# A routed block's last three expert tiles behind a branch, and another order of combining

## The chip, the core and the metric

The kernel runs on one core of a Trainium2 chip. The metric is the device time of one launch in microseconds. TensorE (PE; its weight loads are PEld) multiplies, VectorE (DVE) and ScalarE (ACT) do the elementwise work and read PSUM, GpSimd (POOL) does elementwise work in SBUF and issues the indirect DMAs, SyncE (SP) issues all other DMAs.

## The reference

A transformer block in float32 with a modulation by a condition vector: layer norm, attention with 16 heads, a residual, layer norm again, then a mixture of experts with a shared expert beside it. x has 4 batches of 512 tokens of 512 features. Cut to what matters:

```python
x = x + ga * attn(layernorm(x) * (1 + ca) + sa)
h = layernorm(x) * (1 + cb) + sb                  # 2048 tokens x 512
scores = softmax(h @ gate_weight.T)               # 8 experts
topk_w, topk_idx = top_k(scores, 2)               # two experts a token
topk_w = topk_w / (sum(topk_w) + 1e-20)
y  = sum over the two experts of topk_w * (silu(h @ wg.T) * (h @ wu.T)) @ wd.T   # F = 352
y += (silu(h @ sg.T) * (h @ su.T)) @ sd.T                                        # shared, FS = 704
x = x + gb * y
```

## The kernel before

**Sorting by expert.** The attention part fills the first two thirds of the time and is left as it is. While it runs, `route(b)` finds each token's two experts and scatters the token's row to `xs` in DRAM, which has a region for each expert; `xs` was filled with zeros before, in 15 pieces (line 1151, `xs<-nothing`), one after each head from the second on. At the end `plan_tiles` counts the tokens of each expert and cuts each expert's region into tiles of 128 rows. `ends[e]` is the running sum of tiles over the experts; `expert_of[i]` and `row_of[i]` say which expert's weights and which row of `xs` tile i takes. 4096 rows in 8 groups need at most 39 tiles (`NT`), and the program always runs 39: tiles behind the counted ones take the last expert and rows of zeros, and nobody reads what they give.

**A tile.** `load_in(i)` reads the expert's number into a register of SP and loads its gate and up weights into `wgu[i % 2]` (line 1418), `load_down(i)` its down weights into `wdn[i % 2]` (line 1434); both are conditional: where tile i has the expert of tile i - 2 nothing is loaded. `load_rows(i)` loads 128 rows. On PE `tile_in` transposes them (pxt, line 1443), `tile_hidden` multiplies by gate and up (pgt and put, line 1456), ACT and DVE make the product of silu and up, `tile_turn` transposes it (pht, line 1472), `tile_down` multiplies by the down weights (pyt, line 1483), ACT copies the result to `yt` (line 1491), and `keep(i)` writes it to `ys` in DRAM (line 1495). The loop is pipelined by hand: in pass i PE gets tile i's hidden products, tile i + 1's transposes, tile i - 1's down and tile i's second transposes, so that ACT and DVE work on one tile while PE works on another.

**The shared expert.** It runs in two halves of two batches, one before the tiles and one behind them. Each half begins with `shared_tail` for both of its batches (64 of the hidden columns that don't fit the blocks: pst, line 1204, then a silu on ACT, line 1212, and two products on DVE, line 1215, into `hid`), goes on with `shared_hidden` for five blocks (w_s, line 1229) and ends with `shared_down` for each of its two batches (w_d, line 1310). Hidden and down products use seven products in place of eight (`seven`); each is taken from PSUM by DVE or ACT before its bank can be used again. These banks, the tag "w", are three in number; pst and the tiles' pgt use the same three. In the second half a down's quadrants are added to the residual on DVE, multiplied by gb and sent to the output from there (lines 1332 to 1336).

**Combining.** `combine(n, bt)` takes a block of 128 tokens: `fetch` gathers its two rows from `ys` by indirect DMAs on POOL, four blocks ahead. For batches 0 and 1 the two rows are weighted and multiplied by gb and added to the residual, by ACT (line 1529), DVE (1531, 1532) and POOL (1533), and SP sends the block (`finish`, line 1499). For batches 2 and 3 two DVE instructions (1525, 1527) add the weighted rows to a residual that has been divided by gb ahead of time, and it goes out later, with the second half's downs. The combining is a generator of two steps a block, woven between the steps of the second half's products: 24 steps during the hidden products, 8 during the downs. Batches 0 and 1 share one place in SBUF for their residuals (`xr1`), so batch 1's is loaded when batch 0 has left.

**Order.** PE, DVE, ACT and SP run in the order of the program text (`manual_schedule`); POOL's order is the scheduler's. The pools of the stages ("half1", "tiles", "half2") lie over one another in SBUF: `hid` of the second half lies where `xT`, `ht`, `hTt` and `yt` of the tiles were.

Of the kernel before, what the change touches and what calls it, by code (L numbers as in the profile page):

```python
# [14 lines left out]
P = 128  # L15
# [21 lines left out]
TOPK = 2  # L37
CAP = B * S
NT = TOPK * B * S // P + NE - 1
NFILL = 15  # L40
NROW = NE * CAP + (NE - 1) * P
I32 = mybir.dt.int32
# [6 lines left out]
def adaln_block_kernel(  # L49
# [29 lines left out]
    def bank(tag, name):  # L79
        if tag in ("ps", "pt"):  # L80
            return psum.tile([P, 512], F32, tag=tag, name=name)
        bufs = {"w": 3, "po": 1}[tag]
        return psum2.tile([P, 512], F32, tag=tag, bufs=bufs, name=name)
# [328 lines left out]
    def plan_tiles(shp):  # L412


        late["plan"] = []

        def t(tag, *dims, dt=F32):
            return shp.tile([P, *dims], dt, tag=tag, name=tag)

        def over(a, n):  # L420
            return a.unsqueeze(1).to_broadcast([P, n, a.shape[1]])

        def each(a, n):
            return a.unsqueeze(2).to_broadcast([P, a.shape[1], n])

        pn = bank("pt", "pn")[:, :NE]
        nc.tensor.matmul(pn, lhsT=ones, rhs=seen[:, B * NTB, :], start=True, stop=True)
        count = t("count", NE)
        nc.vector.tensor_copy(count, pn)
        begun = t("begun", NE, B * NTB)  # L430
        nc.vector.tensor_tensor(
            begun, each(count, B * NTB), over(full, NE), ALU.is_gt
        )
        tiles = t("tiles", NE)
        nc.vector.tensor_reduce(tiles, begun, AX.X, ALU.add)
        yield
        upto = t("upto", NE, NE)
        nc.vector.tensor_tensor(upto, ltri, over(tiles, NE), ALU.mult)
        ends = t("ends", NE)
        nc.vector.tensor_reduce(ends, upto, AX.X, ALU.add)  # L440
        yield
        past = t("past", NT, NE)
        nc.vector.tensor_tensor(past, each(tileno, NE), over(ends, NT), ALU.is_ge)
        which = t("which", NT)
        nc.vector.tensor_reduce(which, past, AX.X, ALU.add)
        nc.vector.tensor_scalar_min(which, which, float(NE - 1))
        expert_of = t("expert_of", NT, dt=I32)
        nc.vector.tensor_copy(expert_of, which)
        yield
        step = t("step", NE)  # L450
        nc.vector.tensor_scalar(
            step, tiles, float(-P), float(CAP), op0=ALU.mult, op1=ALU.add
        )
        nc.vector.tensor_tensor(past, past, over(step, NT), ALU.mult)
        nc.vector.tensor_reduce(which, past, AX.X, ALU.add)
        nc.vector.scalar_tensor_tensor(
            which, tileno, float(P), which, op0=ALU.mult, op1=ALU.add
        )
        row_of = t("row_of", NT, dt=I32)
        nc.vector.tensor_copy(row_of, which)  # L460
        late["plan"] = [expert_of, row_of]
        yield

        move = t("move", NE)
        nc.vector.tensor_sub(move, ends, tiles)
        nc.vector.scalar_tensor_tensor(
            move, move, float(P), slot0, op0=ALU.mult, op1=ALU.subtract
        )
        nc.vector.tensor_add(at, at, over(move, B * NTB))
        rows = []  # L470
        late["plan"].append(rows)
        for k in range(TOPK):
            yield
            mine, row, found = t("mine", B * NTB, NE), t("row", B * NTB), t(f"rows{k}", B * NTB, dt=I32)
            nc.vector.tensor_mul(mine, hots[k], at)
            nc.vector.tensor_reduce(row, mine, AX.X, ALU.add)
            nc.vector.tensor_copy(found, row)
            rows.append(found)
# [374 lines left out]
    def load_for_second(b):  # L853

        late["x"] = work.tile([P, NTB, D], F32, tag="xh", bufs=1, name=f"xh_2_{b}")
        nc.sync.dma_start(out=late["x"], in_=x[b].rearrange("(t p) d -> p t d", p=P))
        spread(ga_bc, GA, b)
        late["mod"] = [
            work.tile([P, D], F32, tag=f"rows{k}", bufs=1, name=f"rows{k}_{b}")
            for k in range(2)  # L860
        ]
        spread(late["mod"][0], CB, b)
        spread(late["mod"][1], SB, b)
# [135 lines left out]
    def weave(main, n, fill, count):  # L999

        done = 0
        for k in range(n):
            next(main, None)
            while done * n < count * (k + 1):
                done += 1
                next(fill, None)
# [50 lines left out]
    with tc.manual_schedule(engines={ENG.PE, ENG.DVE, ENG.Activation, ENG.SP}):  # L1057
# [15 lines left out]
        for G in range(NGB):  # L1073
# [14 lines left out]
            for u in range(GH):  # L1088
# [56 lines left out]
                    open_out(b)  # L1145
                if (g, u) == (3, 2):
                    load_for_second(b)

                k, n = GH * G + u - 1, NROW // P // NFILL
                if 0 <= k < NFILL:  # L1150
# [46 lines left out]
    def halves2(a):  # L1197
        return a.rearrange("p b (s n) -> p b s n", s=2)

    def shared_tail(b):  # L1200

        pt = bank("w", f"pst_{b}")
        for c in range(NC):
            nc.tensor.matmul(
                pt,
                lhsT=wst[:, c, :],
                rhs=h2s[b][:, c // 2 * 2 : c // 2 * 2 + 2, c % 2, :],
                start=(c == 0),
                stop=(c == NC - 1),
            )  # L1210
        sg = gate[:, b % 2]
        nc.scalar.activation(sg[FT:, :], pt[:FT, :], AF.Silu)
        for k in range(2):
            rows = slice(FT + k * FT // 2, FT + (k + 1) * FT // 2)
            nc.vector.tensor_mul(
                hids[b // 2 * 2][FT:FL, b % 2, k::2, 1, :],
                halves(sg[rows]),
                halves(pt[rows]),
            )
# [185 lines left out]

    def other(i):

        if i < 2:
            return {}
        return dict(  # L1410
            cond=expert[i] != expert[i - 2]
        )
# [34 lines left out]
        nc.vector.tensor_copy(xT.rearrange("p c s -> p (c s)"), pt)  # L1447
        return xT

    def tile_hidden(i, xT):  # L1450
        pg = bank("w", f"pgt_{i}")
        pu = bank("ps", f"put_{i}")
        for k, ps in enumerate((pg, pu)):
            for c in range(NC):
                at = (k * NC + c) * F
                nc.tensor.matmul(  # L1456
                    ps[:, :F],
                    lhsT=xT[:, c, :],
                    rhs=wgu[i % 2][:, at : at + F],
                    start=(c == 0),  # L1460
                    stop=(c == NC - 1),
                )
        sg = phase[-1].tile([P, F], F32, tag="tsg", name=f"tsg_{i}")
        nc.scalar.activation(sg, pg[:, :F], AF.Silu)
        ht = phase[-1].tile([P, F], F32, tag="ht", name=f"ht_{i}")
        nc.vector.tensor_mul(ht, sg, pu[:, :F])
        return ht
# [26 lines left out]
    def keep(i, yt):  # L1494
        nc.sync.dma_start(out=ys[i * P : (i + 1) * P, :], in_=yt)
# [54 lines left out]
    with tc.manual_schedule(engines={ENG.PE, ENG.DVE, ENG.Activation, ENG.SP}):  # L1550
# [17 lines left out]
        open_phase("half1")  # L1568
        load_xr(0, moe, "xr0")
        open_hidden(0)  # L1570
        shared_tail(0)
        sums_of_b(nc.gpsimd, h2s[0])
        shared_tail(1)
        sums_of_b(nc.vector, h2s[1])

        def slots_found():
# [28 lines left out]
        open_phase("tiles")  # L1605
        turned = {0: tile_in(0, xts.pop(0))}
        flat, ready = {}, divided()
        for i in range(NT + 1):
            if i < NT:
                ht = tile_hidden(i, turned.pop(i))  # L1610
                if i + 2 < NT:
                    load_in(i + 2)
                    xts[i + 2] = load_rows(i + 2)
                if i + 1 < NT:
                    turned[i + 1] = tile_in(i + 1, xts.pop(i + 1))
            if i >= 1:
                yt = tile_down(i - 1, flat.pop(i - 1))
                if i + 1 < NT:
                    load_down(i + 1)
                keep(i - 1, yt)  # L1620
            if i < NT:
                flat[i] = tile_turn(i, ht)
            next(late["steps"], None)
            if i == 4:
                load_h2(2)
                load_h2(3)
            if i >= 6:
                next(ready, None)
            if i == 8:
                most_of_b(nc.gpsimd, h2s[2])  # L1630
                most_of_b(nc.gpsimd, h2s[3])


        open_phase("half2")
        order = [bt for b in (0, 2, 3, 1) for bt in range(b * NTB, (b + 1) * NTB)]
        open_hidden(2)
        load_xr(0, moe, "xr1")
        shared_tail(2)
        shared_tail(3)
        rest_of_b(nc.gpsimd, h2s[2])  # L1640
        rest_of_b(nc.gpsimd, h2s[3])
        for m in range(4):
# [1 line left out]

        def combined():
            for m, bt in enumerate(order):
                if m == 3 * NTB:
                    load_xr(1, moe, "xr1")
                yield from combine(m, bt)
                if m + 4 < len(order):  # L1650
                    fetch(m + 4, order[m + 4])
                yield
# [2 lines left out]
        weave(main, 4, iter(()), 0)  # L1655
        weave(main, NSEV - 6, fill, 6 * NTB)
        weave(main, 5, iter(()), 0)
        weave(main, 2 * SEVEN - 2, fill, 2 * NTB)
        drain(main)
        drain(fill)  # L1660
        parts.close()
# [112 lines left out]
```

## Time and profile before

| | us |
|---|---|
| median of 3 runs | 1808.78 |
| lowest, highest | 1806.71, 1808.8 |
| the profiled execution | 1807.06 |
| its span | 1805.3 |
| first to last tile on TensorE (1372.07 to 1691.16) | 319.1 |
| from there to TensorE's end (1794.82) | 103.7 |
| from there to the end of the span | 10.5 |

A row of the chain of waits gives start, duration and what ran; a row of the timeline gives start, duration, engine, line, operation, output and inputs, count, and in brackets the idle time before it and what ended it. All times are microseconds from the start of the span. Matmul ends are modelled. TensorE's granted clock was 0.99 over the span.

### The profile page before, as it was taken

How to read it: one execution, taken by the hardware profiler on the slowest of the kernel's cores; microseconds unless marked ns; L12 is line 12 of the kernel's file. 1: busy time of each engine (PE TensorE's matmuls, PEld its weight loads, DVE VectorE, ACT ScalarE, POOL GpSimd, SP SyncE). 2: the span in 40 equal slices, each digit the busy share in tenths (PEclk: the TensorE clock that was granted, in tenths of full speed). 3: DMA queues.
4: the chain of work that ended last, by engine and by line, in shares of the span. 5: the costliest groups of instructions: out<-in, count | busy, mean ns of one | idle time of the engine just before them, and what ended most of it. 6: DMA issues, size and time to landing. Idle time of an engine off the chain costs nothing.

```text
span 1805.3 us, 21946 instructions
## 1 busy us (share of the span) xinstructions
PE 1732.3 (96%) x7637; PEld 1319.4 (73%) x7637; DVE 901.6 (50%) x1900; ACT 549.2 (30%) x1321; POOL 587.9 (33%) x702
## 2 busy tenths in 40 slices
PE   6999999998999999899999989999999999999997
PEld 4766777786887888678778867886786565656686
DVE  4554454456556554754554565444683221121397
ACT  1024444204445421544441354443300111111110
POOL 6334662404253312443331456425210110000351
PEclk9999999999999999999999999999999999999999
DMA  6569889636342253434243376436042656554352
GB/s 245 173 207 287 272 287 310 216 137 206 121 152 103 74 171 123 152 115 140 82 143 123 115 238 206 136 125 240 29 164 93 232 197 213 181 183 144 111 152 93
DMA packets 157838, 301.93 MB, mean 167 GB/s; under 512 B 19216, under 2 KB 97552, under 8 KB 151072
## 3 DMA queue, kind: packets, MB, share of 16 engines
q1 hardware_dynamic: 152608, 283.75, 47.2%
q0 software_dynamic: 5120, 16.78, 2.9%
q8 instruction: 61, 1.00, 0.2%
q14 instruction: 49, 0.40, 0.1%
HBM read 254.72 MB, written 97.03 MB: 195 GB/s over the span
## 4 chain that ended last, share of the span: by engine, by line
PE 79%; DVE 8%; POOL 4%; ACT 4%; DMA 2%; issue 2%; SPq 0%; POOLq 0%; ACTq 0%; DVEq 0%
PE w_v L689 10%; PE w_q L603 10%; PE w_o L726 10%; PE w_k L641 7%; PE ps L778 6%; PE po L820 5%; PE pyt L1483 5%; PE pgt L1456 5%; PE put L1456 5%; PE w_s L1229 5%; PE w_d L1310 3%; PE ppt L806 3%; ACT prob L796 1%; DVE xh L260 1%; PE pxt L1443 1%
## 5 line engine op out<-in xcount | busy, mean ns | idle before, releaser
L789 ACT ACTIVATE prob<-ps,nmax 128x128 f32<-128x128 f32 (+3 forms) x256 | 134.2, 525 | 362.2 <-DVE nmax L787 354.4
L641 PE MATMUL w_k<-h,wk 128*128 128x256 f32 x896 | 223.0, 387 | 5.3 <-ACT p_k L653 2.7
L726 PE MATMUL w_o<-wo,oS 128*128 128x256 f32 x896 | 208.9, 379 | 0.0
L689 PE MATMUL w_v<-wv,h 128*128 128x256 f32 x896 | 206.1, 379 | 2.0 <-DVE u_q L623 1.3
L603 PE MATMUL w_q<-h,wq 128*128 128x256 f32 x896 | 203.6, 382 | 1.3 <-DVE qT L629 1.3
L603 PEld LDWEIGHTS w_q<-h,wq 128*128 128x128 f32 x896 | 169.9, 191 | 27.8 <-issue 3.4
L641 PEld LDWEIGHTS w_k<-h,wk 128*128 128x128 f32 x896 | 165.6, 195 | 28.0 <-ACT p_k L653 5.8
L689 PEld LDWEIGHTS w_v<-wv,h 128*128 128x128 f32 x896 | 167.3, 190 | 24.0 <-DVE u_q L623 1.7
L726 PEld LDWEIGHTS w_o<-wo,oS 128*128 128x128 f32 x896 | 164.6, 190 | 21.3 <-issue 1.4
L778 PE MATMUL ps<-kT,qT 128*128 128x128 f32 (+3 forms) x512 | 174.6, 442 | 1.4 <-ACT prob L789 1.2
L820 PE MATMUL po<-probT,v 128*128 128x512 f32 (+3 forms) x512 | 151.7, 436 | 13.1 <-DVE probT L814 13.0
L820 PEld LDWEIGHTS po<-probT,v 128*128 128x128 f32 x512 | 95.1, 190 | 71.2 <-issue 30.2
L806 PEld LDWEIGHTS ppt<-ident,prob 128*128 128x128 f32 x640 | 83.4, 143 | 82.7 <-issue 36.1
L796 ACT ACTIVATE prob<-prob,rsum 128x128 f32<-128x128 f32 (+3 forms) x256 | 122.8, 551 | 63.7 <-DVE rsum L793 62.7
L739 POOL TENSOR_TENSOR xres<-xres,p_o 128x512 f32<-128x512 f32 x48 | 60.9, 1270 | 212.6 <-DVE xres L739 118.7
L787 DVE TENSOR_REDUCE nmax<-ps 128x1 f32<-128x128 f32 (+3 forms) x256 | 125.8, 491 | 8.8
L1229 PE MATMUL w_s<-h2s,ws 128*128 128x256 f32 x560 | 124.5, 381 | 4.5 <-DVE h2s L497 1.4
L806 PE MATMUL ppt<-ident,prob 128*128 128x128 f32 x640 | 109.9, 280 | 15.0 <-ACT prob L796 12.1
L1229 PEld LDWEIGHTS w_s<-h2s,ws 128*128 128x128 f32 x560 | 105.3, 190 | 21.7 <-DVE h2s L497 1.8
L1483 PE MATMUL pyt<-wdn,hTt 128*128 128x512 f32 (+1 forms) x234 | 107.0, 593 | 0.6 <-ACT yt L1491 0.6
L785 DVE TENSOR_TENSOR ps<-ps,cmask 128x128 f32<-128x128 f32 x256 | 75.1, 293 | 59.7 <-PE ps L778 47.9
L1456 PE MATMUL pgt<-wgu,xT 128*128 128x352 f32 x312 | 100.4, 465 | 2.5 <-DVE xT L1447 2.4
(285 smaller groups left out, 2325.4 us busy)
## 6 DMA issues: line engine op xcount, KB each, us to landing
wgu<-in_wexp_dram SPq DMA_DIRECT2D x39, 1408.0 KB
xs<-nothing SPq DMA_DIRECT2D x15, 2304.0 KB
wdn<-in_wexp_dram SPq DMA_DIRECT2D x39, 768.0 KB
wo<-sums_o SPq DMA_DIRECT2D x12, 1536.0 KB
wq<-sums_q SPq DMA_DIRECT2D x24, 640.0 KB
wk<-sums_k SPq DMA_DIRECT2D x24, 640.0 KB
wv<-sums_v SPq DMA_DIRECT2D x12, 1280.0 KB
xt<-xs SPq DMA_DIRECT2D x39, 256.0 KB
```

What stands on the lines that cost most here:

```text
L603: nc.tensor.matmul(dst, lhsT=w[:, sa, c, :], rhs=h7[b][:, sb_, c, :], start=c == 0, stop=c == 1,)
L641: nc.tensor.matmul(dst, lhsT=w[:, sa, c, :], rhs=h7[b][:, sb_, c, :], start=c == 0, stop=c == 1,)
L689: nc.tensor.matmul(dst[:, t2 * HW : (t2 + 1) * HW], lhsT=h7[b][:, sb_, c, t2 * P : (t2 + 1) * P], rhs=w[:, sa, c, :], start=t2 == 0 and c ...
L726: nc.tensor.matmul(dst[:, t2 * HW : (t2 + 1) * HW], lhsT=oSs[hp][:, sa, t2 * P : (t2 + 1) * P], rhs=w[:, hp, sb_, :], start=t2 == 0 and hp ...
L778: nc.tensor.matmul(ps[:, :n], lhsT=qT[:, q0 : q0 + P], rhs=kT[:, u % 2, :n], start=True, stop=True,)
L789: nc.scalar.activation(blk, ps[:, :n], AF.Exp, bias=nmax, accum_out=rsum[:, i : i + 1])
L796: nc.scalar.mul(blk, blk, rsum[:, k : k + 1])
L806: nc.tensor.transpose(pt[:, at : at + P], prob[:, QO[i] + j * P : QO[i] + (j + 1) * P], ident,)
L820: nc.tensor.matmul(po[:, j * P :], lhsT=v()[:, j, u * DH : (u + 1) * DH], rhs=probT[:, KO[j] : KO[j] + (NTB - j) * P], start=(j == 0), sto ...
L1229: nc.tensor.matmul(dst[:, n * HW : (n + 1) * HW], lhsT=ws[k][:, sa, c, :], rhs=h2s[b + n][:, sb_, c, :], start=(n == 0 and c == 0), stop=( ...
L1456: nc.tensor.matmul(ps[:, :F], lhsT=xT[:, c, :], rhs=wgu[i % 2][:, at : at + F], start=(c == 0), stop=(c == NC - 1),)
L1483: nc.tensor.matmul(py, lhsT=hT_t[:fn, k, :], rhs=wdn[i % 2][:fn, k * D : (k + 1) * D], start=(k == 0), stop=(k == len(FCH) - 1),)
```

## The change

It has four parts.

1. The loop runs over `NA` = 36 tiles in place of 39. The number of tiles counted (`ends` of the last expert) is kept as an integer, read into a register of every engine in pass 12, and the last three tiles stand in a branch, `tc.If(used > NA)`, behind the loop. In the branch they run one after the other, not pipelined, with loads that are not conditional and one PSUM bank for the three gate products.
2. The rows of `ys` that belong to those three tiles are filled with zeros early, by a DMA of SP in the attention part (group 1, first head), beside the zeros for `xs`.
3. `shared_tail` is cut in two: `tail_products`, PE's part, which for the second half now stands before the last tile's down, and `shared_tail`, which stays where it was, behind the branch.
4. The combining goes by batches 0, 2, 1, 3 in place of 0, 2, 3, 1. Batch 1's residual is loaded at block 6 of 16 in place of block 12, and the last 8 steps are woven into the 5 steps from the middle of the first of the last two downs, in place of 12 steps over both.

```diff
@@ -37,6 +37,7 @@
 NT = TOPK * B * S // P + NE - 1
+NA = NT - 3
 NFILL = 15
@@ -459,6 +460,9 @@
         late["plan"] = [expert_of, row_of]
+        used = t("used", 1, dt=I32)
+        nc.vector.tensor_copy(used, ends[:, NE - 1 :])
+        late["used"] = used
         yield
@@ -1145,6 +1149,11 @@
                     load_for_second(b)
+                if G == 1 and u == 0:
+                    nc.sync.dma_start(
+                        out=ys[NA * P :, :].rearrange("(p n) (c w) -> p (n c) w", p=P, w=P),
+                        in_=nothing.unsqueeze(1).to_broadcast([P, (NT - NA) * NC, P]),
+                    )
@@ -1197,7 +1206,7 @@
-    def shared_tail(b):
+    def tail_products(b):
 
         pt = bank("w", f"pst_{b}")
         for c in range(NC):
...
+        return pt
+
+    def shared_tail(b, pt):
         sg = gate[:, b % 2]
         nc.scalar.activation(sg[FT:, :], pt[:FT, :], AF.Silu)
@@ -1405,7 +1417,7 @@
     def other(i):
 
-        if i < 2:
+        if i < 2 or i >= NA:
             return {}
@@ -1447,8 +1459,8 @@
-    def tile_hidden(i, xT):
-        pg = bank("w", f"pgt_{i}")
+    def tile_hidden(i, xT, pg=None):
+        pg = bank("w", f"pgt_{i}") if pg is None else pg
@@ -1605,20 +1617,22 @@
-        for i in range(NT + 1):
-            if i < NT:
+        for i in range(NA + 1):
+            if i < NA:
                 ht = tile_hidden(i, turned.pop(i))
...
+            if i == NA:
+                tails = [tail_products(b) for b in range(half, B)]
             if i >= 1:
                 yt = tile_down(i - 1, flat.pop(i - 1))
-                if i + 1 < NT:
+                if i + 1 < NA:
                     load_down(i + 1)
                 keep(i - 1, yt)
...
+            if i == 12:
+                used = nc.values_load(late["used"][0:1, 0:1], min_val=0, max_val=NT)
             if i == 8:
                 most_of_b(nc.gpsimd, h2s[2])
                 most_of_b(nc.gpsimd, h2s[3])
 
+        with tc.If(used > NA):
+            pg = bank("w", "pgt")
+            for i in range(NA, NT):
+                load_in(i)
+                xt = load_rows(i)
+                load_down(i)
+                ht = tile_hidden(i, tile_in(i, xt), pg)
+                keep(i, tile_down(i, tile_turn(i, ht)))
 
         open_phase("half2")
-        order = [bt for b in (0, 2, 3, 1) for bt in range(b * NTB, (b + 1) * NTB)]
+        order = [bt for b in (0, 2, 1, 3) for bt in range(b * NTB, (b + 1) * NTB)]
         open_hidden(2)
         load_xr(0, moe, "xr1")
-        shared_tail(2)
-        shared_tail(3)
+        shared_tail(2, tails[0])
+        shared_tail(3, tails[1])
         rest_of_b(nc.gpsimd, h2s[2])
         rest_of_b(nc.gpsimd, h2s[3])
@@ -1644,7 +1669,7 @@
             for m, bt in enumerate(order):
-                if m == 3 * NTB:
+                if m == NTB + 2:
                     load_xr(1, moe, "xr1")
@@ -1655,7 +1680,7 @@
         weave(main, NSEV - 6, fill, 6 * NTB)
         weave(main, 5, iter(()), 0)
-        weave(main, 2 * SEVEN - 2, fill, 2 * NTB)
+        weave(main, SEVEN - 2, fill, 2 * NTB)
         drain(main)
```

More of the change, by code (lines that the diff above doesn't have):

```diff
@@ L1570, in adaln_block_kernel @@
         open_hidden(0)
-        shared_tail(0)
+        shared_tail(0, tail_products(0))
         sums_of_b(nc.gpsimd, h2s[0])
-        shared_tail(1)
+        shared_tail(1, tail_products(1))
         sums_of_b(nc.vector, h2s[1])
@@ L1607, in adaln_block_kernel @@
         flat, ready = {}, divided()
-        for i in range(NT + 1):
-            if i < NT:
+        for i in range(NA + 1):
+            if i < NA:
                 ht = tile_hidden(i, turned.pop(i))
-                if i + 2 < NT:
+                if i + 2 < NA:
                     load_in(i + 2)
                     xts[i + 2] = load_rows(i + 2)
-                if i + 1 < NT:
+                if i + 1 < NA:
                     turned[i + 1] = tile_in(i + 1, xts.pop(i + 1))
+            if i == NA:
+                tails = [tail_products(b) for b in range(half, B)]
             if i >= 1:
                 yt = tile_down(i - 1, flat.pop(i - 1))
-                if i + 1 < NT:
+                if i + 1 < NA:
                     load_down(i + 1)
                 keep(i - 1, yt)
-            if i < NT:
+            if i < NA:
                 flat[i] = tile_turn(i, ht)
```

## The prediction

> **What bounds the kernel now.** I read the page first, then the chain of waits, then the timeline of the two places that the change touches: the end of the expert tiles and the end of the kernel. The page and the end of the chain:
>
> ```profile
> span 1805.3 us, 21946 instructions
> PE 1732.3 (96%) x7637; PEld 1319.4 (73%) x7637; DVE 901.6 (50%) x1900; ACT 549.2 (30%) x1321; POOL 587.9 (33%) x702
> q8 instruction: 61, 1.00, 0.2%
> ...
> 1671.95 0.11 PE pht L1472
> 1672.06 2.37 PE pgt L1456 x8
> 1674.43 2.37 PE put L1456 x8
> 1676.80 0.44 PE pxt L1443 x4
> 1677.23 2.58 PE pyt L1483 x6
> 1679.81 0.33 PE pht L1472 x3
> 1680.14 2.37 PE pgt L1456 x8
> ...
> 1687.47 0.02 issue
> 1687.49 0.59 ACT yt L1491
> 1688.09 0.26 issue
> 1688.35 2.81 PE pyt L1483 x6
> 1691.16 6.87 PE pst L1204 x16
> 1698.03 60.43 PE w_s L1229 x280
> 1758.46 28.58 PE w_d L1310 x132
> ```
>
> TensorE is the bound: 1732.3 of 1805.3 us, and from 1698.03 to 1787 the chain is TensorE alone. A tile begins at 1672.06 and the next at 1680.14, so a tile costs 8.08 us of TensorE, back to back. Work taken from TensorE here shortens the kernel one for one, if nothing new makes it wait.
>
> The end is different. TensorE stops at 1794.82, the kernel runs on to 1805.3:
>
> ```profile
> 1792.06 2.76 PE L1310 MATMUL w_d<-sdn,h2s 128*128 128x256 f32 x12
> 1795.81 0.69 DVE L1335 TENSOR_TENSOR xres<-xres,gb_bc 128x512 f32<-128x512 f32 x1
> 1796.41 0.75 DVE L1531 SCALAR_TENSOR_TENSOR y_sb<-y_sb,cw 128x512 f32<-128x512 f32 x1
> 1797.19 0.69 DVE L1532 TENSOR_TENSOR y_sb<-y_sb,gb_bc 128x512 f32<-128x512 f32 x1
> 1797.96 1.26 POOL L1533 TENSOR_TENSOR xr<-xr,y_sb 128x512 f32<-128x512 f32 x1 [7.47 <-DVE y_sb L1532]
> 1799.25 0.34 SPq L1499 DMA_DIRECT2D out_dram<-xr  x1
> ```
>
> The last thing sent is not a shared down but the last block of batch 1's combine; the last down is ready at 1796.50.
>
> **Is the branch skipped?** The change gains its three tiles only if at most 36 are counted. Evaluating the reference on its inputs gives, for the eight experts, 566, 621, 515, 510, 528, 444, 433 and 479 tokens: 5, 5, 5, 4, 5, 4, 4, 4 tiles of 128, which is 36, so "used > 36" is false. The trace agrees as far as it can. SyncE's weight load of a tile (L1418) is issued for every tile, in 0.33 us where the expert changed and 0.08 where it is skipped:
>
> ```profile
> 1620.26 0.33 SPq L1418 DMA_DIRECT2D wgu<-in_wexp_dram  x1
> 1628.34 0.33 SPq L1418 DMA_DIRECT2D wgu<-in_wexp_dram  x1
> 1636.42 0.09 SPq L1418 DMA_DIRECT2D wgu<-in_wexp_dram  x1
> ```
>
> The long ones are those of tiles 5, 6, 10, 11, 15, 16, 19, 20, 24, 25, 28, 29, 32 and 33: the tile starts that those counts give. The last expert starts at tile 32; that it ends at 35 rests on its 479 tokens, since tiles behind the count read the same expert.
>
> **The change part by part** (minus is faster).
>
> 1. Three tiles leave TensorE: 3 x 8.08 = -24.2 us. With them go 3 row loads, 3 result writes, and what ScalarE and VectorE do for them, all under TensorE.
>
> 2. The shared tails' 16 matmuls (pst, 6.87 us) move ahead of the last tile's down. Their time stays. In the old order TensorE waited from 1687.47 to 1688.35 for ScalarE before the last down; 6.87 us of tails now stand there: -0.9.
>
> 3. The seam behind the last down is new. Before, pst also covered what follows that down: the copy of yt (0.59), the write to ys (issued 1691.8 to 1692.12, landed by 1694.29, when POOL's memset of hid starts without a wait: at most 2.2 us), the Silu (0.59) and two products of each tail (1.39). Now pst is over before the down, and Silu and products stand behind the branch in ScalarE's and VectorE's own order. They write hid, which lies over the pool that yt is in, and the gate in wgu[1], which the arm would load: they have to know that the arm and the last write are over. Call the down's end T. Copy, issue and landing end at T + 3.1 at the latest; Silu and products free the first of the two w banks that pst holds at about T + 5.6 with half a us of branch, the second 1.4 later. There are three w banks. If the shared stage's first product gets the third one at once, its second is due at about T + 2 and loses 3.5; if the banks go strictly round, the first waits and 5.6 are lost. No row of this trace shows a branch. Low end: nothing waits for the write, loss 0.7. High end: all engines stop, about 10. I take 5, near the two cases worked out from rows.
>  [...]
>
> 4. The register load of the count in iteration 12, on each engine. SyncE's own rows: 0.27 us a TENSOR_LOAD, 0.15 the operations behind it, 0.02 an assertion. In TensorE's order it stands between transposes and a hidden product, where its sequencer may be ahead: 0 to 0.5, I take +0.2. On the others 0.45 us lies in idle time (ScalarE waits 4.9 us for each pyt). The copy of the count (one VectorE instruction of a column) lies beside the shared downs: nothing.
>
> 5. The zero write to the last three tiles of ys, 0.79 MB, issued by SyncE beside the xs zeros of about 164.67, for some 0.6 us of its queue. The DMA engines carry 256 GB/s there at a share of 0.82, so it is 3 us of their time; 18% of 20 us is free, and TensorE is busy 20.00 of 20 in both stretches to 200. The next weight load behind it (wv) is issued at 177.68. Zero; without that slack at most 3, at the wo load at 198.53, whose chain already holds TensorE about 2 us.
>
> 6. The new order. Up to the downs VectorE has as many instructions as before: 2 a block. ScalarE gets 4 multiplies of 0.73 and POOL 4 additions of 1.27 from batch 1 in a stretch of 60.43 us where they are busy 11.41 and 38.41. SyncE reloads batch 1's residual at block 6 rather than 12; it must wait until batch 0's four results have left, sent some 4 us before, and has about 12 us for its 1 MB before POOL adds to it: 0, at most 2.
>  Batch 3's eight VectorE instructions of 0.75 fall into the first down and the start of the second. VectorE is busy 13.52 of 18.02 us in the first down, 0.75 of that batch 1's; seven of the eight in its place make 18.0, all of it. Following it product by product with these durations, its lag is largest at the first down's last product, whose w bank comes free at about 1782.3 where TensorE wants it at 1781.67: with the signal 0.7 us of stall. Then batch 1's work is gone from the second down (4 of its 16.88) and VectorE catches up.
>  At the end the send of the last down, ready at 1796.50, takes the place of that at 1799.25: -2.75. Together -2.0; bounds -2.75 and +2 (the stall three times as long, and the end unchanged).
>
> Sum: -24.2 - 0.9 + 5.0 + 0.2 + 0 - 2.0 = -21.9. The profiled execution took 1807.06 us, 1805.3 of it span: 1785.2. The median of the runs shown is 1808.78, 1.7 higher; I put the forecast between the two bases, at 1786.0.
>
> **The rivals.**
> - The arm runs (37 or more counted; the nearest such count is three tokens more for the fourth expert, 34 for the last). Its loads are unconditional: 2.43 MB a tile, 9.9 us at the 244 GB/s of the busiest 50 us of the tile stage, so 30 for three, some 8 for the last tile's own chain, which nothing overlaps, and the seam: 43 in place of 24.2, with the rest 1823. Slower. Against it: the counts above; the smallest gap between a second and a third logit in the reference is 2.8e-4, of a float32 sum. Chance 0.05.
> - The seam is a full stop: every engine drained, code fetched again, tails and gathers begun only then. 12 us in place of 5: 1793. For it: SyncE cannot pass before the write has landed, and ScalarE, VectorE and POOL all wait for SyncE's count. Chance 0.16.
> - The seam is nearly free and the end gains fully: 0.7 and -2.75: 1781. Chance 0.10.
> - The first down stalls TensorE for what the end gains: 1788, inside the range. Chance 0.06.
> - The forecast as summed: 0.63.
>
> **How the numbers follow.** Unknown costs of the likeliest case: seam 1 to 9, order -2.75 to 0, the base 1.7 either way: 1781.5 to 1791. The range reaches a little into the full stop: 1781 to 1793. A change under 0.2%, 3.6 us, can't be told from none. All cases but the arm's lie far from that: faster 0.93, same 0.01, slower 0.06.
>
> **What would show it.** pgt, put and pyt counts falling from 312, 312, 234 to 288, 288, 216; SyncE's weight loads 36; pst directly before the last pyt with no gap; a hole on TensorE of 4 to 6 us after it, released by VectorE's hid product; a wait of under 1 us at the second down's third product; the last send a down (L1336), about 2 us after TensorE's end. Wrong: counts unchanged, a hole over 10 us at the seam, or a VectorE lag that reaches the last product.

## The result, and the profile after

| | before | after |
|---|---|---|
| median, us | 1808.79 (4 runs, 1806.71 to 1809.43) | 1781.59 (4 runs, 1778.45 to 1783.91) |
| ratio of after to before | | 0.985, 95% interval 0.9831 to 0.987 |
| profiled execution, us | 1807.06 | 1783.91 |
| its span, us | 1805.3 | 1782.2 |

The change is 1.5% faster (1.3 to 1.7). The forecast was 1786.0, range 1781 to 1793. The page of after:

```profile
span 1782.2 us, 21702 instructions
PE 1710.5 (96%) x7550; PEld 1305.8 (73%) x7550; DVE 898.9 (50%) x1892; ACT 545.6 (31%) x1312; POOL 589.5 (33%) x702
```

Its answers by tile and by line, each row a line, engine and operation with its count, shortest, median and longest duration in ns and first and last start: the gate products, the reading of the count, the branch, and the signals behind it:

```profile
L1468 PE MATMUL pgt<-wgu,xT x288: 459/459/563, 1374.3 to 1658.8; 128*128 128x352 f32 x144
L1644 PEldq TENSOR_LOAD <-used x1: 487/487/487, 1476.5 to 1476.5; - x1
L1649 PEldq COMPARE_BRANCH  x1: 363/363/363, 1666.1 to 1666.1; - x1
L1649 SPq EVENT_SEMAPHORE  x9: 17/17/17, 1675.2 to 1676.9; - x9
```

288 gate products are 36 tiles of 8: the branch was skipped. TensorE reads the count in 0.49 us and branches in 0.36, at 1666.1, while its matmuls of the tails still run. The branch is over at 1666.5, 8.2 us before TensorE's first product behind it (1674.67).

The seam behind the last down, in the timeline (here and in the later fences, rows between those shown are left out):

```profile
1664.34 7.03 PE L1213 MATMUL pst<-h2s,wst 128*128 128x512 f32 x16
1671.20 2.74 PE L1495 MATMUL pyt<-wdn,hTt 128*128 128x512 f32 x6
1673.98 0.59 ACT L1503 COPY yt<-pyt 128x512 f32<-128x512 f32 x1 [8.67 <-PE pyt L1495]
1674.67 1.99 PE L1241 MATMUL w_s<-h2s,ws 128*128 128x256 f32 x8 [0.72 <-ACTq L1649]
1676.96 2.81 DVE L1227 TENSOR_TENSOR hid<-wgu,pst 32x512 f32<-32x512 f32 x4 [12.00 <-SPq L1649]
1678.50 6.71 PE L1241 MATMUL w_s<-h2s,ws 128*128 128x256 f32 x30 [1.84 <-DVE hid L1227]
```

The tails stand right before the last down, with no gap. Behind it TensorE waits twice, 0.72 us for ScalarE's signal behind the branch and 1.84 for VectorE's product into hid, which starts when SyncE's last signal at 1676.9 says that the write to ys has landed.

The last hidden block, and the start of the downs:

```profile
1733.58 2.16 DVE L1306 TENSOR_TENSOR ws<-ws,hid 128x512 f32<-128x512 f32 x1
1733.91 1.27 POOL L1545 TENSOR_TENSOR xr<-xr,wdn 128x512 f32<-128x512 f32 x1
1739.17 1.27 POOL L1545 TENSOR_TENSOR xr<-xr,y_sb 128x512 f32<-128x512 f32 x1
1739.44 1.56 DVE L1310 TENSOR_TENSOR ws<-hid,ws 128x512 f32<-128x512 f32 x1
1739.63 3.70 PE L1322 MATMUL w_d<-sdn,hid 128*128 128x256 f32 x16 [1.24 <-issue]
1744.18 2.00 PE L1322 MATMUL w_d<-sdn,hid 128*128 128x256 f32 x8 [0.85 <-DVE hid L1282]
```

VectorE's additions L1306 and L1310 take 2.16 and 1.56 us beside POOL's additions of batch 1; other instructions of their shape take 0.68. TensorE waits 1.24 and 0.85 us in consequence, where before it ran without a gap (e9 below tests the cause).

The end, in the timeline of after:

```profile
1774.58 2.76 PE L1322 MATMUL w_d<-sdn,h2s 128*128 128x256 f32 x12
1777.62 0.68 DVE L1346 TENSOR_TENSOR xres<-xres,w_d 128x512 f32<-128x512 f32 x1
1778.33 0.69 DVE L1347 TENSOR_TENSOR xres<-xres,gb_bc 128x512 f32<-128x512 f32 x1
```

By line, the drains that POOL and SyncE make at the end, first of after, then of before:

```profile
L1795 POOLq DRAIN  x3: 40/112/6660, 1740.5 to 1781.9; - x3
L1795 SPq DRAIN  x3: 7/7/13, 1781.3 to 1781.6; - x3
```
```profile
L1770 POOLq DRAIN  x3: 40/107/6615, 1797.9 to 1805.1; - x3
L1770 SPq DRAIN  x3: 7/7/13, 1801.7 to 1804.8; - x3
```

POOL's long drain takes 6.6 us in both. Before, it began at 1797.9, with POOL's last addition, and ended 2.8 us behind the start of SyncE's first, 1801.7, by when SyncE's data had landed. Now it begins at 1740.5 and lies under the downs.

Stage by stage, from the starts of the named matmuls in each profile (us). The time before the first half's first shared tail is left out of the sums: it varied between 1248.6 and 1255.5 over all kernels profiled here, and by 4.6 between two executions of after, with the same instructions, which is most of the 5.3 us between their spans. It goes with the clock that TensorE was granted: 34.1 us of this part ran at half the clock in the first profile of after, 20.5 in the second. Over the thirteen profiles the time of this part and the time at half the clock have a correlation of 0.88. What halves the clock is not shown.

| stage | before | after | after, second profile |
|---|---|---|---|
| first shared tail to the end of the last tile's down | 440.0 | 420.6 | 420.7 |
| from there to the second shared product (the seam) | 8.6, of it 6.9 pst | 4.7 | 4.7 |
| to the first down | 58.7 | 61.1 | 60.4 |
| the first down | 18.2 | 19.4 | 19.4 |
| the second down, to TensorE's end | 18.3 | 18.3 | 18.3 |
| to the end of the span | 10.5 | 4.9 | 4.9 |
| sum | 554.4 | 529.0 | 528.3 |

1.5 us of the first line's difference are the clock as well. The gate products of the first tile, before and after:

```profile
1372.07 4.14 PE L1456 MATMUL pgt<-wgu,xT 128*128 128x352 f32 x8 [2.40 <-DVE xT L1447]
```
```profile
1374.34 2.63 PE L1468 MATMUL pgt<-wgu,xT 128*128 128x352 f32 x8 [2.40 <-DVE xT L1459]
```

In the 2.5 us from their start TensorE was granted 0.50 of its clock before and 1.00 after. It was 0.50 in e7 and f1 too, which have 36 tiles, and 1.00 in e2, which has 39.

### The profile page after: what moved, and what is told of

It reads as the page before. It is cut to its first block, busy times and chain, and to the rows that moved or that the text cites. A ratio compares the mean times of both kernels' runs of the same rounds, so it can differ in the third digit from the quotient of the medians.

```text
span 1782.2 us, 21702 instructions
## 1 busy us (share of the span) xinstructions
PE 1710.5 (96%) x7550; PEld 1305.8 (73%) x7550; DVE 898.9 (50%) x1892; ACT 545.6 (31%) x1312; POOL 589.5 (33%) x702
## 5 line engine op out<-in xcount | busy, mean ns | idle before, releaser
L693 PEld LDWEIGHTS w_v<-wv,h 128*128 128x128 f32 x896 | 167.3, 190 | 24.9 <-DVE kT L660 2.2
L1495 PE MATMUL pyt<-wdn,hTt 128*128 128x512 f32 (+1 forms) x216 | 98.7, 593 | 0.0
L1478 DVE TENSOR_TENSOR ht<-tsg,put 128x352 f32<-128x352 f32 x36 | 18.8, 521 | 150.0 <-PE put L1468 125.5
```

Of the source, the lines that this page charges most:

```text
L693: nc.tensor.matmul(dst[:, t2 * HW : (t2 + 1) * HW], lhsT=h7[b][:, sb_, c, t2 * P : (t2 + 1) * P], rhs=w[:, sa, c, :], start=t2 == 0 and c ...
L1495: nc.tensor.matmul(py, lhsT=hT_t[:fn, k, :], rhs=wdn[i % 2][:fn, k * D : (k + 1) * D], start=(k == 0), stop=(k == len(FCH) - 1),)
```

## The experiments

All times are medians; ratios are to the kernel before on the same chip. Where a difference is below the spread of the runs, the stages of the profile decide.

**The changed kernel again.**

> The changed kernel once more, as the base of the comparisons that share its chip. By the first trace its 23.1 us of gain are made of -24.2 for the tiles, +0.9 and +1.8 of idle TensorE behind the last down, about +3.9 of short waits for VectorE late in the second half, +0.7 carried over from the attention part, and -5.6 behind TensorE's end. If the waits late in the second half depend on the moment, the runs spread between 1778 and 1784 as the first four did, and a second profile shows other sums there.

1779.53 us, ratio 0.9851 (0.9835 to 0.9868), runs from 1777.68 to 1784.03. The second profile is the last column above: the waits late in the second half are there in both, 0.7 us apart, so they are not what sets the two profiles 5.3 us apart. The part ahead of the first tail is: 1253.2 in the first profile, 1248.6 in the second. The granted clock of the two executions, 0.990 and 0.994, goes the same way.

**The order alone, taken away and put in.**

```diff
# e1: the changed kernel with
-order = [bt for b in (0, 2, 1, 3) ...]        +order = [bt for b in (0, 2, 3, 1) ...]
-if m == NTB + 2:                              +if m == 3 * NTB:
-weave(main, SEVEN - 2, fill, 2 * NTB)         +weave(main, 2 * SEVEN - 2, fill, 2 * NTB)
# e2: the kernel before with the same three lines the other way
```

> The changed kernel with the old order of combining (0, 2, 3, 1), its late reload and its 12 steps. Theory O (batch 1's work, put among the last hidden products, makes VectorE late there): TensorE runs the hidden products and downs without the 3.9 us of waits; the end is 10.5 us behind TensorE's end again instead of 4.9. Together +1.7 over the changed kernel. Rival S (the waits come from the seam: the gathers start later against the products because the tails no longer cover them): the waits stay, the end is lost: +5.6.

> The kernel before with the new order of combining alone, 39 tiles and no branch. Theory O: the waits of about 3.9 us late in the second half appear here too, the end is 4.9 us behind TensorE's end: 1.7 faster than before. Rival S: no such waits: 5.6 faster. The prediction's own figure for this part was 2.0 faster.

e1 took 1786.15 us, ratio 0.9873 (0.9857 to 0.9889). In its stages the hidden products and first down are back at 58.8 and 18.2, the end at 10.55: 531.2 in all, 2.2 to 2.9 more than the changed kernel. By the medians of the runs it is 6.6 more, which alone would point to S; the part ahead of the first tail, with 41 us at half the clock in e1's profile, enters there, so the stages decide. e2 took 1805.53, ratio 0.9989 (0.9982 to 0.9996): 2.0 us faster than before, between 0.7 and 3.3. Its stages are 60.3, 19.4 and 5.15. The waits come and go with the order, with or without branch: theory O holds, S falls. The order's net is 2.0 us by the runs; in the stages it is 2.6, +2.8 in front of TensorE's end and -5.4 behind it.

The end follows POOL's drain. In e1:

```profile
L1795 POOLq DRAIN  x3: 40/113/6613, 1777.5 to 1784.7; - x3
L1795 SPq DRAIN  x3: 7/7/13, 1781.0 to 1784.4; - x3
```

It starts again with the last addition, at 1777.5, and outlasts SyncE's.

**No branch.**

```diff
-if i == 12: used = nc.values_load(...)
-with tc.If(used > NA): ...          # the arm goes too
```

> The changed kernel with 36 tiles and neither branch nor the count's register loads; it computes what the changed kernel computes on these inputs. Theory W (behind the last down the engines wait for the landing of the last write to ys, and the branch itself costs only the 0.9 us before the first shared product): 0.5 to 1 faster than the changed kernel, VectorE's first product into hid still some 3 us behind the down's end. Rival B (the branch is what holds them): 2.7 faster, TensorE without a gap.

1778.88 us, ratio 0.9845 (0.9831 to 0.9859), not to be told from the changed kernel by the runs. By the stages 526.85, 1.4 to 2.1 less. Its seam:

```profile
1669.29 1.89 PE L1241 MATMUL w_s<-h2s,ws 128*128 128x256 f32 x8
1671.86 1.99 PE L1241 MATMUL w_s<-h2s,ws 128*128 128x256 f32 x8 [0.68 <-ACT wgu L1265]
1672.56 2.81 DVE L1227 TENSOR_TENSOR hid<-wgu,pst 32x512 f32<-32x512 f32 x4 [12.09 <-DMA ys<-yt]
```

The down ends at 1669.30. VectorE's product starts 3.26 us behind it, in the changed kernel 3.17: there the branch adds nothing, the write's landing sets it, as theory W has it. TensorE gains 0.9 before the first shared product and 1.2 before the second, which waits for ScalarE's copy of the first and not for hid; probably the three banks go round differently without the arm's, which was not tested by itself. About 1 us is given back in the hidden products (61.7). The tile stage is 0.5 us shorter, but not where the count is read: the gate products of tiles 10 to 14 start 8.08 us apart in every profile, with the count or without. What e3 lacks is short waits for a tile's rows at tiles 24 and 28, and before and e2, which read no count, have them too (0.24 and 0.47). Without these 0.5 the branch costs 0.9 to 1.6 us by one profile, about what W expected or somewhat more, and less than B.

**The arm runs.**

```diff
-with tc.If(used > NA):
+with tc.If(used > NA - 1):
```

> The changed kernel with the branch taken: used > 35 in place of used > 36, so that the three tiles behind the 36 counted run in the arm. This is the prediction's first rival as an experiment: it puts the arm at 38 us behind the loop (30 for 7.3 MB of weights and rows, 8 for the last tile's own chain), and the kernel at 1823. If the loads of the arm's first two tiles start while the loop's last tiles run, or the tiles overlap, it is nearer to the 24.2 us of the pipelined tiles: 1804.

With `used > 35` the arm runs, with `used > 36` it did not, so exactly 36 tiles are counted. 1850.09 us, ratio 1.0244 (1.0223 to 1.0264): 43 slower than before, and far over the 1823 of the prediction's rival. From the end of the loop's last down (1672.45) to that of the arm's last (1740.48) it is 68.0 us, 22.7 a tile. The chain shows why:

```profile
1675.42 5.88 DMA xt<-xs
1681.43 1.10 PE pxt L1455 x4
1683.30 5.06 PE pgt L1468 x8
1688.37 2.80 PE put L1468 x8
1692.94 2.83 PE pyt L1495 x6
1695.79 0.59 ACT yt L1503
1696.40 0.33 SPq L1507
1697.52 0.33 SPq L1430
1698.63 5.97 DMA xt<-xs
```

A tile's loads are issued behind the tile before's write (L1507, then L1430), since SyncE goes in order and the write waits for the whole tile: nothing overlaps. The rival had the loads of three tiles follow one another at 9.9 us each. Part of the time is the clock: over the three tiles of the arm TensorE was granted 0.72, 0.78 and 0.69 of it, and their eight gate products took 5.06, 4.09 and 4.99 us, where the loop's took 2.37. Neither expectation of the experiment holds.

**One tail on each side.**

```diff
-tails = [tail_products(b) for b in range(half, B)]
+tails = [tail_products(half)]
-shared_tail(3, tails[1])
+shared_tail(3, tail_products(3))
```

> The changed kernel with batch 2's tail products ahead of the last down and batch 3's behind the branch. If the seam's loss is the wait of the second shared product for a bank that the tails hold until the last write to ys has landed, 3.43 us of batch 3's products cover it: the 1.8 us gap goes, the 0.9 before it stays: 2 faster. If batch 3's products or the first shared product now wait for the same bank: no difference.

1780.37 us, ratio 0.9853 (0.9834 to 0.9872): no difference by the runs. By the stages 526.0, 2.3 to 3.0 less:

```profile
1672.34 3.67 PE L1213 MATMUL pst<-h2s,wst 128*128 128x512 f32 x8
1675.19 2.87 DVE L1227 TENSOR_TENSOR hid<-wgu,pst 32x512 f32<-32x512 f32 x4 [8.55 <-SPq L1649]
1675.85 9.44 PE L1241 MATMUL w_s<-h2s,ws 128*128 128x256 f32 x43
```

The second tail runs while the write lands; both waits of the seam are gone but for 0.4 us. The seam's loss was the wait for a held bank, and 3.4 us of TensorE's own work cover it.

**Who makes VectorE late.**

```diff
# e7: batch 1's addition on VectorE                # e9: left out
-nc.gpsimd.tensor_add(x_t, x_t, y2)
+(nc.vector if b else nc.gpsimd).tensor_add(x_t, x_t, y2)
```

> The changed kernel with batch 1's four additions to the residual on VectorE instead of POOL. Theory L (an addition of POOL stretches the VectorE instruction beside it: L1306 took 2.15 us in place of 0.68, L1310 1.56): the time from the second shared product to the second down falls from 79.8 us to about 77, the value of the old order: 2.5 faster than the changed kernel. Rival C (VectorE has too much to do there, whoever adds): four more instructions of 0.69 make the waits longer: 0 to 2 slower.

> The changed kernel without batch 1's four additions: its output lacks the experts' part for batch 1. VectorE has exactly the changed kernel's instructions. Theory L: the waits late in the second half go, 79.8 to about 77 us from the second shared product to the second down. Rival C: they stay at 79.8.

e9: 1779.16 us, ratio 0.9851 (0.9832 to 0.987). Its hidden products take 58.8 us and its first down 18.2, the values of before, and what is left of TensorE's waits behind the tiles is the seam:

```profile
PE w_s L1241 <- DVE hid L1227: 1.8, 1, 1.8
PE w_s L1241 <- ACTq L1650: 0.7, 1, 0.7
```

VectorE had the same instructions. With POOL's four additions away, L1306 and L1310 took 0.68 and 0.73:

```profile
1730.20 0.68 DVE L1306 TENSOR_TENSOR ws<-ws,hid 128x512 f32<-128x512 f32 x1
1734.59 0.73 DVE L1310 TENSOR_TENSOR ws<-hid,ws 128x512 f32<-128x512 f32 x1
```

So theory L: POOL's additions stretch VectorE's. e7: 1781.23, ratio 0.9862 (0.9843 to 0.9881); 60.4 and 18.5, so only 0.9 of the 2.8 us comes back against the second profile of the changed kernel, 1.6 of the 3.5 against the first. Four instructions of 0.69 more cost a good part of what the stretching did. Theory L named the cause, but its number for e7 was wrong, and C has a part: VectorE has little room there.

The stretching itself is not new. In the downs of before:

```profile
1777.13 0.68 DVE L1332 TENSOR_TENSOR xr<-xr,w_d 128x512 f32<-128x512 f32 x1
1777.29 1.27 POOL L1533 TENSOR_TENSOR xr<-xr,wdn 128x512 f32<-128x512 f32 x1 [20.12 <-DVE wdn L1532]
1777.84 1.26 DVE L1334 TENSOR_TENSOR xr<-xr,h2s 128x512 f32<-128x512 f32 x1
```

Beside POOL's eight additions, five VectorE instructions were stretched before (1.92, 1.24, 2.46, 1.26 and 1.20 us) and five after (1.51, 2.46, 2.47, 2.16 and 1.56). All ten read both inputs from SBUF; those with an input in PSUM (w_d or w_s), such as L1332 above, kept their 0.68. Before, TensorE ran on without a gap. What the new order adds is the place: the last three of the five lie late in the hidden products, where the downs wait for VectorE's sums.

By the records the two of the last hidden block end behind POOL's additions: L1306 0.56 us behind the end of the one beside it (1735.18), L1310 0.56 behind the end of its one (1740.44), near the 0.68 and 0.73 that they take in e9, as if most of each had run only then. That it did is not shown. Which of the two starts first makes no difference in these records: L1306 starts 0.33 us before the addition, L1310 0.27 behind it, and both are stretched.

**Putting it together.**

```diff
# f1: one tail on each side, batch 1's additions on VectorE
# f2, f3: one tail on each side, and the 24 steps end 2 or 4 product steps earlier, ahead of VectorE's sums
-weave(main, NSEV - 6, fill, 6 * NTB)          +weave(main, NSEV - 8, fill, 6 * NTB)     # f3: NSEV - 10
-weave(main, 5, iter(()), 0)                   +weave(main, 7, iter(()), 0)              # f3: 9
```

> One tail on each side of the last down, and batch 1's additions on VectorE. The changed kernel takes 528.3 to 529.0 us from the first shared tail of the first half to the end (the attention part before it varies by 5 us from execution to execution, so the stages are compared). If the two edits add up: 2.2 and 0.9 less, 525.5. If the additions on VectorE only move the wait: 526.1, as with one tail alone.

> One tail on each side, and the 24 steps of combining woven into 27 product steps in place of 29, so that batch 1's end moves away from the last hidden block, where VectorE also makes the sums for the down. If only that meeting makes VectorE late: up to 2.9 less than one tail alone, 523.5. If POOL (24 gathers of 1.25 and 8 additions of 1.28 us, 40 us in 47) can't follow: more waits, over 526.

> The same with 25 product steps: POOL has 40 us of work in 43. If it can still follow: 523.5 or a little less; if not, waits for the gathers show on ScalarE and VectorE, and 526 or more.

| | median | ratio to before | stages from the first tail | hidden, first down |
|---|---|---|---|---|
| f1 | 1779.96 | 0.9843 (0.983 to 0.9856) | 526.2 | 60.3, 18.5 |
| f2 | 1777.62 | 0.9835 (0.9821 to 0.9848) | 525.1 | 60.7, 18.5 |
| f3 | 1778.50 | 0.9839 (0.9826 to 0.9852) | 523.6 | 59.9, 18.2 |

f3 comes out where it was expected, with a first down without waits and 0.5 us of waits listed in the hidden products. f2 lies halfway. f1's sum has the half clock at the first tile in it, 1.4 us (its second tile starts 128.8 us behind the first tail, for 127.4 in e8); at the full clock the sum would be about 524.8, an estimate: 1.2 below one tail alone, where 0.9 was expected of the additions on VectorE. The run itself does not show it. f3 beats the changed kernel by 4.7 to 5.3 us in the stages; by the runs the two intervals overlap, so that is shown by one profile only.

## Why the prediction was right or wrong

It was right in direction and near in size, 4.4 us of 1781.59 too high, and of its rivals none happened: the one that names 1781 got there by a seam of 0.7 and an end of -2.75, and neither was so. That the number came so near is in part luck: about 2 us too many at the seam and 3 at the end stand against 2.2 to 2.9 too few for VectorE, and the profile of before had 1.5 us of slow clock that no term names. Its terms against what was measured, before the attention part's variation:

| step | forecast | measured |
|---|---|---|
| 1, 2, 4: tiles, gap, reading the count | -24.9 | -26.3, of it -1.5 from the clock at the first tile, which is no part of the change; -24.8 without it |
| 3: the seam | +5.0 | +3.0 |
| 5: zeros in ys | 0 | none to be told: the attention part is 1251.0 and 1252.7 without them, 1248.6 to 1255.5 with, and the clock alone moves it by more than the 3 us put as the most |
| 6: waits for VectorE | +0.7 | +2.9 to +3.6 |
| 6: the end | -2.75 | -5.7 |

- **Three tiles.** Right: 36 tiles, the gap before the last down gone. The count took 0.49 us of TensorE's sequencer and held up no product that shows: 0, the low end of 0 to 0.5, not 0.2.
- **The seam.** The mechanism was right: the write's landing holds VectorE's product into hid until T + 3.2 (T + 3.1 forecast), the tails hold two banks, and the first shared product gets the third. The term was mis-sized: working it out gave 3.5 for that case, 5 was taken to stand between two cases. The first of the held banks came free at T + 4.6, not T + 5.6. The half us put for the branch had no row; it took 0.36 us of TensorE's sequencer and 0.05 of ScalarE's and of SyncE's. The rival's full stop, 12 us, was the author's estimate and did not come: TensorE's two waits there are 2.56 us together.
- **The order.** The net, -2.0, was right (e2: -2.0 by the runs, -2.6 in the stages), but by luck: both of its terms were wrong, and their errors cancel. The step that failed is "up to the downs VectorE has as many instructions as before": it counted instructions and not that POOL's four additions come to lie beside VectorE's sums. e9, without them, has none of the waits. The stall that was forecast in the first down did not appear as such: the first down's loss comes from what the hidden block left behind.
- **The end.** The forecast let only the send move. It took the 6.05 us from the last send to the end of the span for the landing. SyncE's data had landed 2.45 us after that send; the rest was POOL's drain, which hangs on POOL's last instruction and not on the last send. With POOL's work over early both go: -5.7.
- **The arm.** Its cost was undersized: 38 us and a seam in the rival, 68 and a seam measured, for it was costed by bandwidth where the chain of load, tile and write sets it, at a clock of 0.69 to 0.78.

## What to carry to other kernels

When work is moved between instructions of another engine, count also which instructions of other engines it will lie beside: the same VectorE instruction, L1306, took 2.16 us beside POOL's addition and 0.68 without it (e9). In the kernel before, five stretched instructions of 1.20 to 2.46 us made TensorE wait nowhere; in the new place TensorE waits 1.24 and 0.85 us. When stages are compared, look at the granted clock of each first: 1.5 us of the tile stage were the clock. Where a pool or a PSUM bank is handed from one stage to the next, leave TensorE work of its own size in the handover, as with one tail on each side: 3.4 us of products there, 2.3 to 3.0 us less in the stages. Skipped, the branch cost 0.9 to 1.6 us here by one profile; the arm that ran took 68.0 us, 22.7 a tile unpipelined, where the loop's tiles take 8.08: look at how often it will run before making it simple.

## What the hardware showed that was not expected

- POOL's drain at the end of the program lasted 6.6 us (6613 to 6661 ns) in ten of the thirteen profiles, and 7.8 to 9.4 in e7, e9 and f1, where POOL has no addition among its last instructions. Its record begins 0 to 1.1 us ahead of that of POOL's last instruction, and it decided the end of the kernel where that instruction was late. What it does is not shown.
- A branch over 174 of TensorE's instructions (three tiles of 29 matmuls and 29 weight loads) took 0.36 us of its sequencer where they were skipped, and was over 8.2 us ahead of the first product behind it; it took 0.09 where they ran (e4).
- The same program's attention part took 1248.6 us in one execution and 1253.2 in another, with 20.5 and 34.1 us of it at half the clock.
- Eight gate products took 2.6 us at the full clock and 4.1 to 5.1 where half of it was granted for some or all of them.
